# Attention's chunk loop: a chunk's loads and an inverse's loads issued one per slot instead of all in a row

## The chip, the cores and the metric

The kernel runs on one core of a Trainium2 chip. The metric is device time in microseconds (us), the median of the runs. The core has five instruction streams that matter here: TensorE (PE in the profile, with its weight loads as PEld), VectorE (DVE), ScalarE (ACT), GpSimd (POOL) and SyncE (SP), which issues most of the DMAs. Each stream works through its own instructions in order and waits on semaphores for the others.

## The reference

Two layers, each of the form x = x + mixer(LN(x)) * silu(ffn(LN(x))), on x of 2 x 1024 x 512 in float32. The change lies in the mixer of the first layer, a gated delta rule with 16 heads of 128:

```python
q = silu(conv(x @ Wq)); k = silu(conv(x @ Wk)) * 128**-0.5; v = silu(conv(x @ Wv))
alpha = sigmoid(x @ Wa + ba); beta = sigmoid(x @ Wb + bb)
def step(S, qt, kt, vt, at, bt):          # per batch and head, 1024 steps in time
    err = S @ kt - vt
    S = at * S - bt * outer(err, kt)
    return S, S @ qt
o = layernorm(o) * ln_w + ln_b
out = (o * sigmoid(x @ Wg)) @ Wo
```

The first layer's ffn has ternary weights. The second layer has a linear recurrence as its mixer and an ffn with 4-bit weights.

## The kernel before

**Chunks.** The recurrence over time is cut into 8 chunks of 128 steps. The 16 heads form 8 groups of 2; a group with both batches is 4 streams, which are worked on together. A pair of a group and a chunk is a unit, and there are 64 units. `units` (L1012) sets their order: two groups alternate, chunk by chunk, so u=0, 1, 2, 3 are (group 0, chunk 0), (1, 0), (0, 1), (1, 1), and u=16 starts groups 2 and 3, u=32 groups 4 and 5, u=48 groups 6 and 7.

**What a unit needs.** Within a chunk, the step from time to time becomes the inverse of a triangular 128 x 128 matrix, of which four 32 x 32 blocks lie on the diagonal. `ahead_k`, `ahead_e` and `ahead_l` (L671 to L726) make the keys, the decays and the triangular matrices of a group some time ahead and store them in DRAM (dk, de, dl). `invert` (L728) inverts all diagonal blocks of one group at once: it loads the blocks from dl into ll with four DMAs (L732), clears m (ml), takes 31 steps of two VectorE instructions each (tl and ml), copies the result back to ll on ScalarE in four pieces, and stores it to dl with four DMAs (L759). It is a generator: each `yield` is a place where it is left and taken up later.

`within` (L765) prepares a unit, one step ahead of its use. It loads k (tile kb, L771), four blocks of G (tile ground, L775), the decays e (tile eb, one buffer, L777) and the row decays eg (L561, called from L781), seven DMAs on SP's queue one after the other. Then GpSimd makes kg and qg, TensorE makes pk and pqk, and VectorE makes kd and at from them. GpSimd also sets eg's first column, ahead of its load.

`across` (L806) is the chain of a unit: VectorE makes rt from v and the product pks of the state, TensorE turns it (pr), and four blocks follow one another: a product zw, a subtraction rr on VectorE, a product with G, a copy w4 on ScalarE. The copies go on into wt with four DMAs for each of the first three blocks (L853, one slot later); the fourth block is copied by VectorE. The product pst of kd and wt then updates the state. `finish` (L881) makes the output po of a unit, and its normalisation.

**What sets the order.** The loop at L1096 makes one step per unit. In each step, `weave` (L1014) runs through 10 slots. A slot counts `order["slot"]` up by one, takes one step of one of two chains (the unit before in even slots, this unit in odd ones), runs what is due in this slot, and then gives TensorE its share of the other work: projections such as pwk, pwq, pwv and pgate, the products of `within` and of `ahead_l`. `later(n, ...)` (L578) puts steps off: the first by n slots, each further one by one slot more; outside the loop, when `order["loop"]` is false, it runs them at once. `Ordered` (L124) keeps this order on TensorE, VectorE, ScalarE and GpSimd. The DMAs on SP are not kept in it: a scheduler places them in SP's queue.

An inverse runs over seven steps of the loop. L1113 starts one at each u that is a multiple of 8 up to 40, for the group that comes two later, and L1117 to L1119 take it up in slots 1, 8, 9 and 10 of that step and in slots 1, 3, 5, 6, 8 and 10 of the next six. These are 40 times in all. Before the change, the first of them issues the four loads and clears m, three do nothing, 31 take the steps, four copy, and the 39th stores.

Steps are of unequal length on TensorE. In steps with u mod 4 below 2, a second projection (`tail`, L1148) is the keys of a later group, up to u=37; at u=40 and 41 there is none, and from u=44 on it is a piece of the output product for as long as that lasts.

Of the kernel before, what the change touches and what calls it, by code (L numbers as in the profile page):

```python
# [22 lines left out]
P = 128  # L23
# [7 lines left out]
NS = 4  # L31
# [25 lines left out]
def cols(ap, n):  # L57

    if len(ap.shape) == 2:
        ap = ap.unsqueeze(2)  # L60
    return ap.to_broadcast([ap.shape[0], ap.shape[1], n])
# [231 lines left out]
def first_layer(ctx, tc, a, cst, minus_half, keep, xnT, od, gd, pd, then):  # L293
# [29 lines left out]
    nc = tc.nc  # L323
# [223 lines left out]
    gr, egr = (dr.tile([NCOL, P], F32, name=n, bufs=1) for n in ("gr", "egr"))  # L547
# [10 lines left out]
    def rows(src, hg, c, dst):  # L558

        col = c * H * B + hg * NS  # L560
        nc.sync.dma_start(  # L561
            dst, src[col : col + NS, :].rearrange("s t -> (s t)").unsqueeze(0).to_broadcast([P, NS * P])
            .rearrange("p (s t) -> p s t", s=NS)
        )
# [6 lines left out]
    order = {"loop": False, "slot": 0}  # L571
# [6 lines left out]
    def later(n, *steps):  # L578


        for i, step in enumerate(steps):
            if order["loop"] and n + i:
                due.setdefault(order["slot"] + n + i, []).append(step)
            else:
                step()

    def mm(out, **kw):
        PE.matmul(out, **kw)

    def turn(out, src):  # L590
        PE.transpose(out, src, ident)
# [136 lines left out]
    def invert(hg, store):  # L728

        ll = pl.tile([P, 32, 32], F32, tag="ll", name=f"ll_{hg}")  # L730
        for bl in range(4):
            nc.sync.dma_start(  # L732
                ll[32 * bl : 32 * bl + 32],
                store["l"][:, :, :, SLOT[bl], :].rearrange("c s i t -> (c s) i t"),
            )
        m = pl.tile([P, 32, 32], F32, tag="ml", name=f"ml_{hg}")
        POOL.memset(m, 0.0)
        POOL.memset(m.rearrange("p i j -> p (i j)")[:, 0 : 32 * 32 : 33], 1.0)
        for _ in range(3):
            yield  # L740
        for i in range(31):
            shape = [P, 31 - i, i + 1]
            t = pl.tile([P, 256], F32, tag="tl", name=f"tl_{hg}_{i}", bufs=2)
            tv = t[:, : (31 - i) * (i + 1)].rearrange("p (t j) -> p t j", j=i + 1)
            DVE.tensor_tensor(
                tv,
                ll[:, i, i + 1 :].unsqueeze(2).to_broadcast(shape),
                m[:, i, : i + 1].unsqueeze(1).to_broadcast(shape),
                ALU.mult,
            )  # L750
            rest = m[:, i + 1 :, : i + 1]
            DVE.tensor_tensor(rest, rest, tv, ALU.subtract)
            yield

        for i in range(0, 32, 8):
            ACT.copy(ll[:, :, i : i + 8].rearrange("p j i -> p i j"), m[:, i : i + 8])
            yield
        for bl in range(4):
            nc.sync.dma_start(  # L759
                store["l"][:, :, :, SLOT[bl], :].rearrange("c s j i -> (c s) j i"),  # L760
                ll[32 * bl : 32 * bl + 32],
            )
        yield

    def within(hg, c, store):  # L765

        u = f"{hg}_{c}"
        half = slice((c % 2) * P, (c % 2 + 1) * P)
        q = windows[hg, c // 2]["q"][:, :, half]
        k = pools["b"].tile([P, NS, P], F32, tag="kb", name=f"kb_{u}")  # L770
        nc.sync.dma_start(k, store["k"][c // 2][:, :, half])  # L771
        G = pools["g"][:, units.index((hg, c)) % 3]
        for s in range(NS):
            r = slice(32 * s, 32 * s + 32)
            nc.sync.dma_start(G[r, :, r], store["l"][c, s])  # L775
        e = pools["b"].tile([P, NS, P], F32, tag="eb", name=f"eb_{u}", bufs=1)
        nc.sync.dma_start(e, store["e"][c])  # L777

        eg = pools["b"].tile([P, NS, P + 4], F32, tag="eg", name=f"eg_{u}", bufs=3)
        POOL.memset(eg[:, :, 0:1], 1.0)  # L780
        rows(egr, hg, c, eg[:, :, 1 : P + 1])  # L781
        kg = pools["b"].tile([P, NS, P], F32, tag="kg", name=f"kg_{u}")
        qg = pools["b"].tile([P, NS, P], F32, tag="qg", name=f"qg_{u}", bufs=3)
        later(
            5,
            lambda: POOL.tensor_tensor(kg, k, eg[:, :, 0:P], ALU.mult),
            lambda: POOL.tensor_tensor(qg, q, eg[:, :, 1 : P + 1], ALU.mult),
        )
        yield 0
        pk = pools["i"].tile([P, NS, P], F32, tag="pi", name=f"pk_{u}")  # L790
        for s in range(NS):
            turn(pk[:, s, :], k[:, s, :])

        kd = pools["b"].tile([P, NS, P], F32, tag="kd", name=f"kd_{u}", bufs=3)
        later(1, lambda: DVE.tensor_tensor(kd, pk, cols(e[:, :, P - 1 : P], P), ALU.mult))
        yield 4 * TURN

        pqk = pools["a"].tile([P, NS, P], F32, tag="pa", name=f"pqk_{u}")
        for s in range(NS):
            mm(pqk[:, s, :], lhsT=k[:, s, :], rhs=q[:, s, :], start=True, stop=True)  # L800
        at = pools["b"].tile([P, NS, P], F32, tag="at", name=f"at_{u}", bufs=3)
        later(1, lambda: DVE.tensor_tensor(at, pqk, e, ALU.mult))
        parts[hg, c] = eg, qg, kg, at, kd, G
        yield 4 * NARROW
# [156 lines left out]
    for hg in range(3):  # L961
        stores[hg] = new_store(hg)
        wk = load_weights(hg, ("wk",))
        steps = invert(hg - 1, stores[hg - 1]) if hg else iter(())
        for p in range(NP):
            for step in of_e:
                step()
            some(1)
            done(ahead_k(hg, p, wk["wk"], stores[hg]))
            loads, *of_e = ahead_e(hg, p, stores[hg])  # L970
            of_e = itertools.chain(*of_e)
            for step in loads:
                step()
            some(1)
            ell()
            for _ in zip(range(0 if hg and not p else 14), steps):
                pass
            ls.append((hg, p))
# [52 lines left out]
    with tc.issue_after(last["act"].ins):  # L1031
# [3 lines left out]
        done(made(0, 0, "v"))  # L1035
        done(made(1, 0, "q"))
        done(within(0, 0, stores[0]))
        halves = sorted(pd)

# [56 lines left out]
        for u in range(len(units) + 1):  # L1096
# [15 lines left out]
            if u % 8 == 0:  # L1112
                steps = invert(slot + 2, stores[slot + 2]) if slot + 2 < HG else none  # L1113
                if slot + 3 < HG:
                    wk = load_weights(slot + 3, ("wk",))
                    stores[slot + 3] = new_store(slot + 3)
# [12 lines left out]
            if u + 1 < len(units):  # L1129
                hg, c = units[u + 1]  # L1130
                ready = within(hg, c, stores[hg])
                other(ready, 1)
# [4 lines left out]
            if turn4 in (0, 2) and ls:  # L1137
                hg, i_ = ls[turn4 // 2]
# [596 lines left out]
```

## Time and profile before

| | |
|---|---|
| median of 3 runs | 3189.33 us (3189.05 to 3189.89) |
| profiled execution | 3191.48 us, of which the span is 3188.9 us |
| window of the chunk loop, from the span's start | about 400 to 1770 us |
| TensorE busy in that window | 1355.53 of 1370 us |
| VectorE, ScalarE, GpSimd busy in it | 965.44, 682.88, 372.22 us |
| DMA share in it | 0.43, 117 GB/s |
| DMA ll<-dl | 128 KB, 32 of them, 4.2 us from issue to landing |
| DMA ground<-dl | 40 KB, 256 of them, 2.3 us |
| DMA wt<-w | 16 KB, 768 of them, 2.0 us |
| DMA kb, eb, eg | 256 KB, 64 each, 3.5, 3.0 and 3.9 us |

The profile shows one execution. Its times are counted from the start of the span, and the median of the runs is 2.15 us below the time of the profiled execution. Busy TensorE is no proof of peak speed, since the ends of matmuls are modelled. A group of instructions is named by its line and by the tiles that it writes and reads (out<-in). Nearly all computing instructions have line 132, since a helper records them, so they are told apart by their tiles. In a list in order of time, a number in brackets is the idle time of the engine ahead of an instruction, with what ended it; SPq is SP's DMA queue.

### The profile page before, as it was taken

The numbers are of one execution on the slowest core, as the hardware profiler recorded it, in microseconds if no ns is written. First come the engines' busy times: TensorE is split into PE (matmuls) and PEld (weight loads), VectorE is DVE, ScalarE is ACT, GpSimd is POOL, SyncE is SP. The second block draws the span as 40 slices with busy tenths as digits, with TensorE's granted clock in tenths as the row PEclk, the third lists the DMA queues.
The fourth block names the chain that finished last, engine by engine and source line by source line (L and its number), as shares of the span: only waits on it lengthen the run. The fifth ranks groups of instructions, "written<-read, shape, count | busy, mean of one in ns | idle before, by whom it ended". The sixth has DMA issues, their size and how long they took to land.

```text
span 3188.9 us, 38235 instructions
## 1 busy us (share of the span) xinstructions
PE 3148.8 (99%) x12454; PEld 1950.8 (61%) x12454; DVE 2147.2 (67%) x4294; ACT 1251.4 (39%) x2269; POOL 832.4 (26%) x1210
## 2 busy tenths in 40 slices
PE   8999999999999999999999999999999999999998
PEld 6576756666666666666666644555555555555554
DVE  4557678786877878675554454677777666776676
ACT  3466555555555555434333200222222222322223
POOL 2000123222322222222222210332333333333222
PEclk9999999999999999999999999999999999999999
DMA  6244344444444443443334465010001000110014
GB/s 183 64 119 113 112 125 115 115 129 126 119 111 132 135 125 109 111 128 100 87 84 142 117 194 156 30 34 27 27 27 40 27 27 27 34 33 27 27 37 132
DMA packets 499494, 287.40 MB, mean 90 GB/s; under 512 B 207328, under 2 KB 440544, under 8 KB 499296
## 3 DMA queue, kind: packets, MB, share of 16 engines
q1 hardware_dynamic: 490432, 268.97, 29.9%
q0 software_dynamic: 6560, 11.80, 1.3%
q10 hardware_dynamic: 2304, 4.20, 0.4%
q8 instruction: 99, 1.62, 0.2%
q14 instruction: 99, 0.81, 0.1%
HBM read 183.90 MB, written 88.34 MB: 85 GB/s over the span
## 4 chain that ended last, share of the span: by engine, by line
PE 76%; DVE 5%; issue 2%; ACT 1%; DMA 1%; SPq 1%; POOL 0%; DVEq 0%; ACTq 0%; POOLq 0%
PE po L132 15%; PE pua L132 7%; PE pga L132 7%; PE pgate L132 6%; PE pwq L132 5%; PE pwv L132 5%; PE pwk L132 4%; PE zw L132 4%; PE pgc L132 3%; PE puc L132 3%; PE jpo L211 3%; PE pub L132 2%; PE pgb L132 2%; PE pr L132 2%; PE pks L132 1%
## 5 line engine op out<-in xcount | busy, mean ns | idle before, releaser
L132 DVE TENSOR_TENSOR acc<-acc,po 128x512 f32<-128x512 f32 x408 | 277.9, 681 | 208.7 <-PE po L132 207.9
L132 PEld LDWEIGHTS po<-w_d,i 128*128 128x128 f32 x1024 | 194.5, 190 | 142.6 <-issue 111.2
L132 PE MATMUL po<-w_d,i 128*128 128x256 f32 (+1 forms) x1024 | 275.4, 392 | 0.0
L132 PE MATMUL pgate<-xnT,wg 128*128 128x512 f32 x512 | 245.7, 593 | 0.0
L132 PE MATMUL pwq<-xnT,wq 128*128 128x512 f32 x512 | 245.1, 593 | 0.0
L132 PE MATMUL pwv<-xnT,wv 128*128 128x512 f32 x512 | 243.0, 594 | 1.8 <-ACT gate L132 1.8
L132 PE MATMUL pua<-xq,w_u 128*128 128x512 f32 x512 | 240.6, 592 | 0.0
L132 PE MATMUL pga<-xq,w_g 128*128 128x512 f32 x512 | 240.6, 592 | 0.0
L132 PE MATMUL pwk<-xnT,wk 128*128 128x512 f32 x512 | 237.6, 596 | 1.5 <-ACT ka L132 1.5
L132 ACT COPY g<-pga 128x512 f32<-128x512 f32 x96 | 56.2, 585 | 447.2 <-PE pga L132 432.8
L132 DVE SCALAR_TENSOR_TENSOR v<-prewv,cw,v 128x512 f32<-128x512 f32 x192 | 165.9, 865 | 63.4 <-ACT v L132 53.3
L132 PEld LDWEIGHTS po<-w_d,s 128*128 128x128 f32 x720 | 136.8, 190 | 95.4 <-issue 77.0
L132 ACT COPY w<-zw 128x128 f32<-128x128 f32 x192 | 50.6, 264 | 362.0 <-PE zw L132 362.0
L132 DVE TENSOR_TENSOR rr<-rr,zw 128x128 f32<-128x128 f32 x192 | 54.6, 284 | 199.2 <-PE zw L132 195.2
L132 PE MATMUL po<-w_d,s 128*128 128x256 f32 x720 | 184.8, 379 | 0.0
L132 ACT ACT_TABLE_LOAD x133 | 170.6, 1283 | 17.9 <-PE pr L132 11.3
L132 POOL TENSOR_TENSOR rs<-rs,minus_half 128x4 f32<-128x4 f32 x64 | 64.5, 1007 | 429.9 <-DVE rs L132 403.8
L132 POOL TENSOR_TENSOR ot<-ot,gate 128x512 f32<-128x512 f32 x64 | 85.9, 1343 | 343.4 <-ACT ot L132 313.7
L132 DVE SCALAR_TENSOR_TENSOR ka<-prewk,cw,ka 128x512 f32<-128x512 f32 x192 | 150.4, 785 | 34.9 <-ACT ka L132 23.2
L132 PEld LDWEIGHTS zw<-rr,ground 128*128 128x128 f32 x512 | 97.0, 191 | 124.5 <-issue 102.4
L132 DVE SCALAR_TENSOR_TENSOR q<-prewq,cw,q 128x512 f32<-128x512 f32 x192 | 159.8, 833 | 15.0 <-POOL eg L132 6.3
L132 PEld LDWEIGHTS zw<-w,ground 128*128 128x128 f32 x768 | 111.3, 192 | 65.6 <-issue 55.2
(248 smaller groups left out, 6661.6 us busy)
## 6 DMA issues: line engine op xcount, KB each, us to landing
e<-gr SPq DMA_DIRECT2D x64, 256.0 KB, 3.9
de<-e SPq DMA_DIRECT2D x64, 256.0 KB, 3.0
dk<-ka SPq DMA_DIRECT2D x32, 512.0 KB, 2.8
kb<-dk SPq DMA_DIRECT2D x64, 256.0 KB, 3.5
eb<-de SPq DMA_DIRECT2D x64, 256.0 KB, 3.0
eg<-egr SPq DMA_DIRECT2D x64, 256.0 KB, 3.9
od<-ot SPq DMA_DIRECT2D x64, 256.0 KB, 2.1
wt<-w SPq DMA_DIRECT2D x768, 16.0 KB, 2.0
```

The source lines that it names most:

```text
L132: i = getattr(self.engine, name)(*args, **kw)
L211: matmul(po, lhsT=ot[:, h, :], rhs=self.wo[h], start=(h == h0), stop=(h == H - 1))
```

## The change

In `invert`, each of the four loads of ll is followed by a `yield` in the loop, and the three empty turns are dropped there: the loads go out in the turns 1 to 4, m is cleared in turn 5 together with the first VectorE step, and the stores go out in turn 40. In `within`, the loads of eg, of e and of the four blocks of G are handed to `later(1, ...)`: eg one slot after k, e two slots after, the blocks three to six slots after. Before the loop both run as they did, in a row, with the row of `within` in the new order.

```diff
@@ invert @@
                 ll[32 * bl : 32 * bl + 32],
                 store["l"][:, :, :, SLOT[bl], :].rearrange("c s i t -> (c s) i t"),
             )
+            if order["loop"]:
+                yield
         m = pl.tile([P, 32, 32], F32, tag="ml", name=f"ml_{hg}")
         POOL.memset(m, 0.0)
         POOL.memset(m.rearrange("p i j -> p (i j)")[:, 0 : 32 * 32 : 33], 1.0)
-        for _ in range(3):
+        for _ in range(0 if order["loop"] else 3):
             yield
@@ within @@
-        for s in range(NS):
+        e = pools["b"].tile([P, NS, P], F32, tag="eb", name=f"eb_{u}", bufs=1)
+
+        eg = pools["b"].tile([P, NS, P + 4], F32, tag="eg", name=f"eg_{u}", bufs=3)
+        POOL.memset(eg[:, :, 0:1], 1.0)
+
+        def block(s):
             r = slice(32 * s, 32 * s + 32)
             nc.sync.dma_start(G[r, :, r], store["l"][c, s])
-        e = pools["b"].tile([P, NS, P], F32, tag="eb", name=f"eb_{u}", bufs=1)
-        nc.sync.dma_start(e, store["e"][c])
-
-        eg = pools["b"].tile([P, NS, P + 4], F32, tag="eg", name=f"eg_{u}", bufs=3)
-        POOL.memset(eg[:, :, 0:1], 1.0)
-        rows(egr, hg, c, eg[:, :, 1 : P + 1])
+
+        later(
+            1,
+            lambda: rows(egr, hg, c, eg[:, :, 1 : P + 1]),
+            lambda: nc.sync.dma_start(e, store["e"][c]),
+            *(functools.partial(block, s) for s in range(NS)),
+        )
```

## The prediction

> **What bounds the kernel.** I read the page first: engines, slices, chain.
>
> ```profile
> span 3188.9 us, 38235 instructions
> ...
> PE 3148.8 (99%) x12454; PEld 1950.8 (61%) x12454; DVE 2147.2 (67%) x4294; ACT 1251.4 (39%) x2269; POOL 832.4 (26%) x1210
> ...
> PEclk9999999999999999999999999999999999999999
> ```
>
> TensorE is busy 99% of the span, at full clock. The change keeps every matmul, in the same order (the built programs agree on that), so only waits of TensorE can be won, with the slow clock behind them. The loop on which the change works runs from about 400 to 1770 us; there the table by stretches gives TensorE 1355.5 us busy of 1370. That is 14.5 us of idle time. Two stretches also run below full clock, 1331.0 to 1337.1 at 0.51 and 1239.9 to 1245.3 at 0.68, which costs 6.1 x 0.49 + 5.4 x 0.32 = 4.7 us. Ceiling of any repair in this loop: 19.2 us, 0.6%.
>
> Next, TensorE's waits in that window, longest first (line, releaser, us in total, times, longest):
>
> ```profile
> PE pst L132 <- DMA wt<-w: 3.5, 1, 3.5
> PE pst L132 <- DVE wt L132: 2.9, 3, 1.7
> PE zw L132 <- DVE rr L132: 1.8, 3, 1.3
> ```
>
> The longest is one wait of the state product pst for the copies wt<-w. The SP queue around it, in order of time (start, us, line):
>
> ```profile
> 1318.01 1.86 SPq L720 DMA_DIRECT2D dl<-lt  x4
> 1320.50 2.70 SPq L732 DMA_DIRECT2D ll<-dl  x4
> 1323.25 3.17 SPq L775 DMA_DIRECT2D ground<-dl  x4
> 1326.52 0.55 SPq L777 DMA_DIRECT2D eb<-de  x1
> 1327.11 0.43 SPq L561 DMA_DIRECT2D eg<-egr  x1
> 1327.64 4.96 SPq L853 DMA_DIRECT2D wt<-w  x8
> ```
>
> and TensorE beside it, then the clock by stretches (us, PE, PEld, DVE, ACT, POOL, clock, DMA):
>
> ```profile
> 1331.02 2.05 PE L132 MATMUL pst<-wt,kd 128*128 128x128 f32 x8 [3.50 <-DMA wt<-w]
> ```
>
> ```profile
> 1331.00:1337.00 6.00, 5.98 (x28) 6.00 (x29) 3.82 (x9) 0.27 (x1) 3.74 (x6) 0.50 0.20 63
> 1337.00:1343.00 6.00, 6.00 (x39) 4.52 (x39) 4.18 (x18) 1.97 (x4) 0.72 (x1) 1.00 0.41 89
> ```
>
> The four ll loads of the last inverse, and a chunk's loads behind them, stand ahead of wt on SP for 7.1 us. TensorE waits 3.5 us, then runs 6 us at half clock. This is chunk step u=40; its slots hold only one projection, so they are short (TensorE's po, which opens a step, comes at 1315.5 and 1336.9).
>
> A second place is at 796 us (u=16): same row, other victim.
>
> ```profile
> 788.89 1.28 POOL L132 TENSOR_TENSOR kg<-kb,eg 128x512 f32<-128x512 f32 x1 [10.33 <-DMA eg<-egr]
> ```
>
> ```profile
> 791.47 2.66 DVE L132 SCALAR_TENSOR_TENSOR ka<-prewk,cw,ka 128x512 f32<-128x512 f32 x2 [4.37 <-POOL prewk L132]
> ```
>
> ```profile
> 795.98 0.49 PE L132 MATMUL zw<-rr,ground 128*128 128x128 f32 x2 [1.35 <-DVE rr L132]
> ```
>
> SP issued eg at 784.84, last of its row. GpSimd, in order, stood at kg; the small copies behind it kept VectorE from ka, and rr came late.
>
> **The change, part by part.**
>
> *The row at u=40.* ll ahead of wt shrinks from four issues to one, ground from four to none; kb comes in between. SP is ordered by a scheduler, and the built order there is ll x1, kb, eg, eb, wt. From 1320.50: 0.61 + 0.61 + 0.43 + 0.55 and gaps, so wt starts at 1322.8 instead of 1327.64. In the trace wt landed 3.25 us after its row began (1330.89), so now at 1326.1. TensorE reaches pst at 1327.52: the 3.50 us go, with 1.4 to spare. With them goes the half clock, 6.1 x 0.49 = 3.0. Together -6.5.
>
> Here a rule of the Trainium skill speaks against the change: "DMA: Bandwidth & Descriptors", section "Issuing engines are not separate DMA queues", says that the sequencer's time to start a DMA is usually small beside the DMA itself. By it, reordering issues would be worth about nothing. The rows say otherwise here: an ll load is 0.61 us to issue and 3.9 to land, wt 0.59 and 1.8, and ten in a row hold wt back from 1320.50 to 1327.64. By the rule this kernel would stay at 3189; I go by the rows.
>
> *The row at u=16.* eg now follows ll x1 (777.32) and kb: issue near 778.9, landing 4.05 later as in the trace, at 783.0; kg starts 5.9 us earlier, VectorE's 4.37 and TensorE's 1.35 go: -1.35. The clock stayed at 1.00 there, so nothing more.
>
> *The loop's start.* kg waited for eg (issued 407.03, landed 411.45), and 10 us later TensorE waited 1.08 for ScalarE's rt behind that chain. eg now goes out about 3.2 us earlier, but kg also moves ahead of small copies in GpSimd's order. Ends 0 and -1.08; I take -0.8, as VectorE's 1.49 wait there for GpSimd is the link that shortens.
>
> *The other chunks.* The number of DMAs is unchanged, so SP's issue time is. Mostly ground moves behind wt. ground is read a whole step later, over 20 us, against 2.3 to land: 0. Without that cover it would cost its 2.3. eb feeds kd five slots later, against 3.0: 0.
>
> *The new wait.* The inverse's loads 2 to 4 now go out in the step's last slots, and its first VectorE step moves from the last slot of the step to the first of the next, behind at. VectorE runs in order; queued behind it are rt (for TensorE's pr) and the next rr. At u=40, SP: wt to 1325.3, ground x3 to 1327.2, wt to 1329.7, ll, ground, ll, ll: the last ll starts near 1331.6 and lands, with 3.9, near 1335.5. VectorE, from 1329.5: state 1.1, three taps of v 2.7, kd 0.7, rr 0.3, at 0.7, so it arrives near 1335.0 and waits 0.5; then 0.4 of inverse and 0.7 of rt: done 1336.6. TensorE wants pr at 1341.46 - 6.5 = 1335.0. That is a loss of 1.6; with the shortest landing in that stretch (3.1) it is 1.1, and I take 1.2. Ends 0 (VectorE early, ll early) and 3.4.
>
> Here the second rule: "TensorE: Matmul & The Clock Gate", Part 1, has the clock halve only after an idle window of about 3.4 us. By it 1.6 costs 1.6. But the row at 1239.9 shows a 1.68 wait followed by a clock of 0.68 for 5.4 us, and 1.35 at 796 by none. So a wait of 1.7 costs 3.4 (the upper end), 1.2 costs 1.2. With the rule the upper end would be 1.7.
>
> At the five other inverses the slots are longer: for u=8 the same count puts the last landing at 612.3 and VectorE there at 615.7: 0. If SP ran 3 us later this cover is gone. GpSimd's clearing of ml (1.17) moves to the same slot, where GpSimd then idles 5 to 9 us: 0. The setting of eg's first column, for which SP's eg waits, comes 1.17 later; wt (2.4) is ahead of eg on SP and covers it. The inverse's stores go out one slot later, 3.04 for four; wt behind them has over 10 us: 0.
>
> *Sum.* -6.5 - 1.35 - 0.8 + 1.2 = -7.45. The profiled execution took 3191.48 (span 3188.9 and 2.6 around it), so 3184.0 for such a run (span 3181.4); the median of the runs before is 3189.33, 2.15 lower, hence **3181.9 us**, -0.23%.
>
> **Rivals.** About 0.2% (6.4 us) is what a measurement of this kernel tells from no change; my gain passes that by 1 us.
>
> *The wait moves one step on.* What leaves the row stands before the next wt. At u=41 the count puts wt at 1337.2, landed 1340.5, and pst is due at 1342.2. If SP is 3.4 us later, pst waits 1.7 and the clock halves: 3.4 back, with 1.6 at pr 3185.7. For: the margin is only 1.7. Against: the count finds SP no earlier event to wait for.
>
> *Hidden anyway, or not done.* SP's order is a scheduler's, and in many steps the built positions are as before. If wt stays late, 3189. Against: the built order at both places has changed.
>
> *Slower: the inverse's first step stalls VectorE.* If the last ll lands over 2.8 us behind VectorE's arrival (TensorE had 4.5 us from pks to pr in step u=9, of which 1.7 is work), pr waits. With 4.5 us, TensorE loses 1.7 and as much by the clock, six times: 20.4 - 8.65 = +11.8, 3201. For: an ll load took up to 6.4 us. Against: the count at u=8 leaves 3.4 us.
>
> **Numbers.** Forecast 0.46; moved on 0.20; hidden 0.12; slower 0.22. Faster by over 0.2%: 0.46; within: 0.32; slower: 0.22. Range 3176 (no new wait, 3180.7, and 4.5 of the other 10.5 us that the ceiling leaves) to 3198 (slower, with five stalls). The forecast's own range is 3177 to 3183.
>
> **What shows it.** Right: no wait of pst for wt near 1327, no half clock until 1337, kg near 783 at u=16, pr waiting under 1.4 near 1335. Wrong: VectorE idle for ll at the inverses, or pst waiting for wt one step on, or other pauses over 1.5 us that halve the clock.

## The result, and the profile after

The changed kernel takes **3184.92 us**, median of 22 runs (3182.42 to 3187.53); the kernel before, in 22 runs beside it, 3189.34 (3186.73 to 3192.11). The ratio is 0.9986 with a 95% interval of 0.998 to 0.9993: 4.4 us less, 0.14%. A second series on another chip gave 3185.07 against 3188.99, ratio 0.9986 (0.9977 to 0.9995). The forecast was 3181.9: the sign is right, the gain is 0.59 of what was forecast. The time lies in the stated range (3176 to 3198) but outside the forecast's own (3177 to 3183), and the gain is within the 0.2% to which the prediction gave 0.32. The profiled execution of the changed kernel took 3185.56.

The page of the changed kernel:

```profile
span 3183.8 us, 38225 instructions
...
PE 3146.3 (99%) x12454; PEld 1948.2 (61%) x12454; DVE 2154.3 (68%) x4294; ACT 1251.3 (39%) x2269; POOL 830.7 (26%) x1210
```

TensorE's count is unchanged and its busy time 2.5 us less. Less slow clock would give about 3.0 (4.7 less in the loop, 1.7 more in the joining stage behind it; both are shown below). The waits of TensorE in the loop (400 to 1770), longest first:

```profile
PE pst L132 <- DVE wt L132: 4.7, 4, 1.7
PE zw L132 <- ACT w L132: 3.5, 7, 1.1
```

and of the kernel before, the row that the prediction does not show:

```profile
PE zw L132 <- ACT w L132: 1.6, 4, 1.0
```

The row "pst <- DMA wt<-w: 3.5" is gone. But "pst <- DVE wt" rose from 2.9 to 4.7, and "zw <- ACT w" from 1.6 to 3.5. In the table by stretches the loop has 12.2 us of idle TensorE (1365 - 1352.8), 14.5 before: 2.3 less. No stretch of the loop is below full clock; before two were, 4.7 us together (5.2 when the stretches are cut at every 5 us, as in the table further down).

The step u=40 on SP (start, us, line), then the engines:

```profile
1316.51 0.57 SPq L732 DMA_DIRECT2D ll<-dl  x1
1317.12 0.67 SPq L773 DMA_DIRECT2D kb<-dk  x1
1317.84 0.62 SPq L561 DMA_DIRECT2D eg<-egr  x1
1318.55 0.45 SPq L787 DMA_DIRECT2D eb<-de  x1
1319.05 2.45 SPq L861 DMA_DIRECT2D wt<-w  x4
1321.59 1.87 SPq L782 DMA_DIRECT2D ground<-dl  x3
```

```profile
1322.19 1.29 POOL L132 TENSOR_TENSOR kg<-kb,eg 128x512 f32<-128x512 f32 x1 [0.39 <-DMA eg<-egr]
1322.26 3.26 DVE L132 SCALAR_TENSOR_TENSOR v<-prewv,cw,v 128x512 f32<-128x512 f32 x2 [3.02 <-ACT v L132]
1323.44 1.54 POOL L132 TENSOR_TENSOR qg<-q,eg 128x512 f32<-128x512 f32 x1
...
1325.55 1.25 DVE L132 COPY wt<-zw 32x128 f32<-32x128 f32 x4
1325.89 1.46 PE L132 MATMUL pst<-wt,kd 128*128 128x128 f32 x8 [1.72 <-DVE wt L132]
```

```profile
1331.00:1337.00 6.00, 6.00 (x34) 4.12 (x33) 4.66 (x21) 1.97 (x4) 1.11 (x2) 1.00 0.52 164
```

SP's order is the forecast one: four issues ahead of wt instead of ten (ll, ground, eb and eg before). wt's DMAs no longer hold pst, and the clock, the third number from the end, stays at 1.00. What holds pst is VectorE's own part of wt, its copies of the fourth block: they are queued behind two taps of v (a tap is one multiply-add of the convolution that makes v), and these take 3.26 us. Before the change the same two took less than half of that:

```profile
1325.61 1.54 DVE L132 SCALAR_TENSOR_TENSOR v<-prewv,cw,v 128x512 f32<-128x512 f32 x2 [3.02 <-ACT v L132]
...
1330.83 1.28 POOL L132 TENSOR_TENSOR kg<-kb,eg 128x512 f32<-128x512 f32 x1 [5.69 <-DMA wt<-w]
```

There GpSimd's kg stood still until TensorE was waiting; now eg is early, and kg and qg run beside the taps. u=32 shows the same: two taps 1.54 before (1145.96), 2.80 after (1142.36), beside kg and qg from 1141.82 to 1144.6, and a new wait of zw of 1.09 at 1150. At u=36 both kernels have it (taps 2.87, pst waits 1.68 before and 1.73 after, near 1237). So the first theory was: **SP's row at u=40 was worth what the profile said, and a part was given back because the early eg lets kg and qg slow VectorE's taps.**

### The profile page after: what moved, and what is told of

Its sections match the earlier page's. It is cut to its first block, busy times and chain, and to the rows that moved or that the text cites. A ratio compares the mean times of both kernels' runs of the same rounds, so it can differ in the third digit from the quotient of the medians.

```text
span 3183.8 us, 38225 instructions
## 1 busy us (share of the span) xinstructions
PE 3146.3 (99%) x12454; PEld 1948.2 (61%) x12454; DVE 2154.3 (68%) x4294; ACT 1251.3 (39%) x2269; POOL 830.7 (26%) x1210
## 4 chain that ended last, share of the span: by engine, by line
PE 88%; DVE 5%; DMA 2%; ACT 2%; issue 2%; SPq 1%; POOL 0%; DVEq 0%; ACTq 0%; POOLq 0%
PE po L132 17%; PE pua L132 7%; PE pga L132 7%; PE pgate L132 6%; PE pwk L132 6%; PE pwq L132 5%; PE pwv L132 5%; PE zw L132 4%; PE pgc L132 3%; PE puc L132 3%; PE jpo L211 3%; PE pu L132 2%; PE pg L132 2%; PE pr L132 2%; PE pub L132 2%; PE pgb L132 2%
```

## The experiments

Every run was timed against the kernel before on its own chip: e1 to e4 on one (before 3188.33, 39 runs), e5 to e8 on one (3190.34, 52 runs), the last three on one (3188.99, 18 runs). Differences are to that median.

**e1, the inverse's half alone** (the diff's part in invert; within as before).

> The kernel before with the inverse's half of the change alone: the four ll loads go out one a slot, a chunk's row (ground, eb, eg) stays in a row. Theory (the gain is the SP row ahead of wt at u=40, and an early eg gives part of it back): three ll issues leave the row there, 1.9 us, so wt begins near 1325.7 and pst waits 1.6 instead of 3.5; eg stays late, so kg and qg don't meet VectorE's taps of v (1.54 us for two, not 3.3), and there are no new waits at u=32. Gain 1.9, up to 4.9 if the half clock goes too, and 0.5 to 1.3 at u=16: 3183 to 3187 us. Rival (the gain lies in the chunk's row alone, ll never mattered): 3189. Rival (VectorE, in order, stands at the inverse's first step for the last ll, so that this half costs): 3190 or more, with a wait of VectorE for ll near 1335.

Measured: 3189.15 us, ratio 1.0002 (0.9994 to 1.001): no gain, the time of the first rival. The rival with VectorE at ll is out, since VectorE has no wait for ll in the trace. pst's wait did shrink, and without a collision:

```profile
1326.85 1.13 PE L132 MATMUL pst<-wt,kd 128*128 128x128 f32 x8 [0.52 <-DMA wt<-w]
```

But rr (0.49) waits right behind it, and five waits of 0.33 to 0.55 for ScalarE's w and v stand elsewhere. The loop has no slow clock in this execution. The loop's idle time is 13.6, so only 0.9 is won, less than the interval can show.

**e2, the chunk's half alone** (the diff's part in within; the inverse as before).

> The kernel before with the chunk's half of the change alone: eg, eb and the four ground blocks go out one a slot, the four ll loads stay in a row. Theory: at u=40 the order on SP is ll x4, kb, eg, eb, wt, so wt begins near 1324.8 and lands near 1328.1; pst waits 0.6 and the half clock goes; eg comes two us later than in the changed kernel, so that kg starts behind the two taps of v and these take 1.54 us. Gain 2.9 + 3.0 at u=40, 1.35 at u=16, 1.2 at the loop's start, less 1 for a collision that stays at u=32: about 3182, that is as good as the whole change or better. Rival (both halves are needed and add up): 3187. Rival (any early eg costs as much as it wins): 3189.

Measured: 3185.55, ratio 0.999 (0.9981 to 0.9998), 2.8 less. About 3182 was expected, and the trace shows one miss: kg did come behind the two taps (1325.23; taps 1.54), yet pst waits.

```profile
1322.06 2.44 SPq L859 DMA_DIRECT2D wt<-w  x4
1322.56 1.54 DVE L132 SCALAR_TENSOR_TENSOR v<-prewv,cw,v 128x512 f32<-128x512 f32 x2 [3.02 <-ACT v L132]
1324.13 1.25 DVE L132 COPY wt<-zw 32x128 f32<-32x128 f32 x4
...
1326.35 1.13 PE L132 MATMUL pst<-wt,kd 128*128 128x128 f32 x8 [1.88 <-DVE wt L132]
```

The row names VectorE, but its first copy was done at 1324.44 (a quarter of 1.25 after 1324.13), 1.9 before pst began. The view of tile wt over 1321.9 to 1324.5, which holds just these four DMAs, gives their times to landing:

```profile
DMA to landing us min/median/max: 2.8/3.5/4.2
```

At 4.2 after 1322.06 one landed at 1326.26, 0.1 before pst began. So it was the DMAs that held pst here; in the trace before, the row's first landed after 3.25.

**e3, the changed kernel with kg and qg two slots later.**

```diff
         later(
-            5,
+            7,
             lambda: POOL.tensor_tensor(kg, k, eg[:, :, 0:P], ALU.mult),
             lambda: POOL.tensor_tensor(qg, q, eg[:, :, 1 : P + 1], ALU.mult),
```

> The changed kernel with GpSimd's kg and qg put two slots later (seven and eight slots behind the step's start instead of five and six), loads as in the changed kernel. Theory (what was given back is VectorE's taps slowed beside kg and qg): the two taps of v near 1322 take 1.54 us instead of 3.26, those near 1142 1.54 instead of 2.80, those near 1234 1.54 instead of 2.87; pst's waits of 1.72 and 1.73 and zw's of 1.09 go: 4.5 us less than the changed kernel, near 3180.4. Rival (the wait of pst near 1326 is a matter of wt's own copies, not of the taps): 3185, pst still waits 1.7. Rival (kg later makes GpSimd's small copies behind it late and pks waits in the next step): 3187 or more.

Measured: **3180.46**, ratio 0.9975 (0.9966 to 0.9983), 7.9 less than before. The time is as expected, the way there only in part: at u=40 only qg moved behind the taps, kg did not.

```profile
1319.85 1.27 POOL L132 TENSOR_TENSOR kg<-kb,eg 128x512 f32<-128x512 f32 x1 [0.38 <-DMA eg<-egr]
1319.93 2.53 DVE L132 SCALAR_TENSOR_TENSOR v<-prewv,cw,v 128x512 f32<-128x512 f32 x2 [3.02 <-ACT v L132]
...
1322.83 1.46 PE L132 MATMUL pst<-wt,kd 128*128 128x128 f32 x8 [1.21 <-DVE wt L132]
...
1325.80 0.49 PE L132 MATMUL zw<-rr,ground 128*128 128x128 f32 x2 [1.08 <-DVE rr L132]
```

At u=40 nothing is won: qg now meets the third tap, rr comes late, and zw waits the 1.08 that the changed kernel does not have. What e3 wins of idle time over the changed kernel lies at other steps: its waits of zw for w are 1.7 in the loop instead of 3.5, and pst's at u=36 is 1.17 instead of 1.73.

**e5, one slot later still** (8 instead of 7).

> The changed kernel with kg and qg three slots later (eight and nine instead of five and six), one slot more than in the run before, where two slots moved only qg behind the taps of v: there the taps took 2.16 to 2.53 us for two, and pst still waited 1.17 and 1.21. Theory (taps slowed beside kg and qg are what was given back): at u=40 kg too comes behind the two taps, which take 1.54; pst's wait near 1322 goes, the one near 1234 as well: 2.4 us less than 3180.5, near 3178. Rival (kg so late is missed by pks at the next step's second slot): waits of TensorE at pks, and 3181 or more.

Measured: 3182.21, ratio 0.9975 (0.9965 to 0.9985), 8.1 less: at u=40 and u=36 the taps are as expected, the time is not better than e3's.

```profile
1321.11 1.54 DVE L132 SCALAR_TENSOR_TENSOR v<-prewv,cw,v 128x512 f32<-128x512 f32 x2 [3.03 <-ACT v L132]
...
1323.02 1.45 PE L132 MATMUL pst<-wt,kd 128*128 128x128 f32 x8 [0.40 <-DVE wt L132]
```

The three runs give the collision's price at three places, as the length of the two taps and the wait of TensorE behind them:

| | u=40: taps, pst waits | u=36: taps, pst waits | u=32: taps, zw waits |
|---|---|---|---|
| changed kernel, kg and qg beside | 3.26, 1.72 | 2.87, 1.73 | 2.80, 1.09 |
| e3, kg beside | 2.53, 1.21 | 2.32, 1.17 | 2.16, 0.45 |
| e5, neither beside | 1.54, 0.40 | 1.54, 0.40 | 1.54, none |

At u=36 the taps shorten by 0.55 and then by 0.78 and the wait by 0.56 and 0.77, at u=32 by 0.64 and the wait by 0.64, one for one; at u=40 the wait shortens by 0.7 to 0.8 of what the taps do. That the taps are what holds these waits is shown. In e5 another wait takes their place, of pr for VectorE's rt (us in the loop, times, longest):

```profile
PE pr L132 <- DVE rt L132: 4.0, 7, 1.1
```

At the longest of them, 1247.94, two taps of ka (3.01 us) ran beside kg and ot, and an instruction of the inverse (1.13 instead of 0.34) beside qg, ahead of rt in VectorE's order. So the collision has moved on in the step; the other six were not traced.

**e6, the later products alone**, in the kernel before (5 to 7 as in e3, the loads in a row).

> The kernel before with kg and qg two slots later (seven and eight), and the loads in a row as they were. It asks whether the 7.9 us of the changed kernel with later products need the change at all. Theory: the row at u=40 still holds wt, so pst's 3.50 stays, and with it the half clock when it comes; eg still goes out last, and kg is late at u=16; only the steps where eg was early enough (near 1237 and behind 1400) win, 0.6 there and 0.3 to 0.7 at two or three more: about 2 less, 3186.5. Rival (the two edits are independent, and the later products alone bring 3.5 to 4.5): 3184.5.

Measured: 3186.26, ratio 0.9986 (0.998 to 0.9993), 4.1 less, more than the expected 2: the sum with the change's 4.4 is 8.5, and together they gave 7.9 (e3). So the rival holds: the two edits are about independent, and what e3 wins over the changed kernel is not a measure of what the change gave back. In this trace the wait of 1.35 at u=16 is gone, the one of 1.04 near 1484 is 0.40, and the one at u=36 is 0.55 shorter. At u=40 the theory was right: the row is untouched, and so is the wait.

```profile
1326.67 2.04 PE L132 MATMUL pst<-wt,kd 128*128 128x128 f32 x8 [4.31 <-DMA wt<-w]
```

```profile
1326.00:1332.00 6.00, 5.33 (x25) 5.36 (x26) 3.18 (x8) 0.27 (x1) 3.92 (x6) 0.50 0.17 56
```

The half clock comes behind it, as in the kernel before.

**e4, the change at one place**: the last inverse of the loop and the chunk (5, 4), both loaded in u=40.

```diff
+            if order["loop"] and hg == 7:
                 yield
...
+        if (hg, c) == (5, 4):
             later(1, ...)
+        else:
+            for s in range(NS):
+                block(s)
+            nc.sync.dma_start(e, store["e"][c])
+            rows(egr, hg, c, eg[:, :, 1 : P + 1])
```

> The kernel before with the change in one place alone: the last of the six inverses in the loop, and the one chunk (group 5, chunk 4) that is loaded in the same step u=40; all other inverses and chunks as before. Theory: the wait of 3.50 becomes one of 1.7 behind the slowed taps and the half clock goes: 1.8 + 3.0, less 0.2, so 3184.7, as the whole change; what the change wins elsewhere (u=16, the start, 2.5) it loses elsewhere (new waits near 1150, 701, 1061, about 2). Rival (the gain is spread over the loop, with a share of each inverse): 3188.5. Rival (the half clock is a matter of luck in one execution, absent from the median): 3187.5.

Measured: 3187.98, ratio 0.9997 (0.9989 to 1.0005). The wait is much as expected (1.43, behind taps of 2.83), and there is no half clock, but the time is that of the two rivals. The loop's idle time is 12.9, 1.6 less than before; the 0.4 us of the median are below even that. The interval reaches to 3.5 us less, just short of the 3.6 expected: that this one step carries the whole gain is not borne out.

**e7, eg ahead of eb and ground, all in a row** (nothing put off).

> The kernel before with the order of a chunk's row alone changed: eg, eb, then the four ground blocks, all in a row as before, the inverse untouched; nothing is put off to other slots. Theory: eg early ends the wait at u=16 (1.35) and shortens the one at the loop's start (0.6), but at u=40 all ten issues are still ahead of wt, so pst still waits 3 us or more near 1327, and kg and qg meet the taps of v: 1.5 to 2.5 less than before, 3186.5. Rival (the early eg is the whole of the gain): 3184. Rival (an early eg costs as much as it wins): 3188.5.

Measured: 3187.56, ratio 0.9989 (0.9983 to 0.9996), 2.8 less, a little more than expected. The waits at u=16 and at the loop's start are gone; pst at u=40 still waits 2.80 for wt, with a clock of 0.72 over the 6 us from 1328. The order alone gives as much as e2 in the median (the intervals are too wide to tell more); ground behind wt is what it lacks. One thing was expected wrongly: kg does not meet the two taps near 1324 there, they take 1.54.

**e8, eg fourth of the six loads.**

```diff
         later(
             1,
-            lambda: rows(egr, hg, c, eg[:, :, 1 : P + 1]),
             lambda: nc.sync.dma_start(e, store["e"][c]),
-            *(functools.partial(block, s) for s in range(NS)),
+            *(functools.partial(block, s) for s in range(2)),
+            lambda: rows(egr, hg, c, eg[:, :, 1 : P + 1]),
+            *(functools.partial(block, s) for s in range(2, NS)),
```

> The changed kernel with eg fourth instead of first of the loads that go out one a slot (eb, two ground blocks, eg, two ground blocks). wt is as free at u=40 as in the changed kernel, only kg starts later, bound to eg's landing. Theory: the taps of v at u=32 and u=40 take 1.54 us again, pst's 1.72 and zw's 1.09 go; against it, GpSimd in order stands at kg for eg in many steps, with the small copies behind it, which costs TensorE 1 to 3 in places like u=16: 3183 to 3186. Rival (the time follows the freeing of wt alone): 3185, with pst's wait of 1.7 unchanged.

Measured: 3187.93, ratio 0.9994 (0.9985 to 1.0002), 2.4 less; not told apart from before, and less than the 3 to 6 expected. At u=40 the taps take 1.54 and pst waits 0.21; but at the loop's start pr waits 2.57, where the changed kernel has 0.26:

```profile
424.02 0.66 PE L132 MATMUL pr<-cst,rt 128*128 128x128 f32 x4 [2.57 <-ACT rt L132]
```

Idle in the loop: 14.2. So eg first instead of fourth is worth 2.3 there alone. The kernel before issued eg as late there (407.03, here 407.17) and waited 1.08; in its order GpSimd clears prewv ahead of kg, here behind it. At u=16 no wait came back. So with pst's wait all but gone the kernel is no faster than the changed one.

**The changed kernel and e3 once more, and e9**: e2 with kg and qg two slots later.

> The changed kernel once more, beside the same with later products on one chip. If the loop's idle time (14.5 to 12.2) and the mean share of slow clock (about 1 us less) are the whole gain: 3 to 4.5 us less than before. The wait of pst near 1326 is 1.7 again, for VectorE's wt; the clock behind it, and behind the fixed wait of 2.70 near 1871, is a matter of the execution.

> The changed kernel with kg and qg two slots later, once more. Theory (two edits that add up: 4.4 for the change, 4.1 for the later products alone): 7.5 to 8.5 us less than before and 3.5 to 4 less than the changed kernel on the same chip.

> The chunk's half of the change alone, with kg and qg two slots later; the inverse's loads stay in a row. Theory: eg lands two us later at u=40 than in the changed kernel, wt is 1.5 us later than there, so pst waits under 1 for it; the chunk alone gave 2.8 and the later products 4.1, so about 6.9 less than before, not better than with the inverse's loads spread (7.9). Rival (spreading ll costs more than it wins once the products are late): 9 less than before.

Measured, in this order: 3185.07, ratio 0.9986 (0.9977 to 0.9995), 3.9 less; 3180.56, ratio 0.9969 (0.9958 to 0.9981), 8.4 less; 3180.59, ratio 0.997 (0.9959 to 0.9981), 8.4 less. The first two are as expected, but e3 is 4.5 below the changed kernel, not 3.5 to 4. e9 misses: 6.9 was expected (its rival said 9, for which e3 beside it would have had to gain less), and pst waits 1.57 and not under 1, again for wt's DMAs (their row began at 1318.72, the longest took 3.5 us, and pst began at 1322.33). e3 and e9 beat both kernels, and are equal: with late products, the spread of ll adds nothing that can be seen (e1 had shown none either).

## Why the prediction was right in sign and too large

All executions together show how far the gain can be accounted for. Idle is TensorE's idle time in the loop, "slow" the time lost there by a clock below 0.97 (summed over stretches of 5 us), both of the profiled execution; "mean clock" is over all the runs of that kernel in its series, each given to 0.001, which is 3.2 us. The sum is an estimate: the idle time less than before, and the mean clock above that of before in the same series (for the changed kernel, above all 109 runs of before), times 3187.

| kernel | pst at u=40 waits | idle | slow | mean clock (of before) | sum | less than before |
|---|---|---|---|---|---|---|
| before | 3.50, DMA | 14.5 | 5.2 | | | |
| e6 | 4.31, DMA | 12.6 | 3.5 | 0.9981 (0.9980) | 2.2 | 4.1 |
| e7 | 2.80, DMA | 11.6 | 3.4 | 0.9981 (0.9980) | 3.2 | 2.8 |
| e2 | 1.88, DMA | 11.4 | 1.7 | 0.9982 (0.9983) | 2.7 | 2.8 |
| changed | 1.72 | 12.2 | 0 | 0.9986 (0.9981) | 3.9 | 4.4 |
| changed, again | 1.76 | 11.8 | 0 | 0.9987 (0.9980) | 5.0 | 3.9 |
| e4 | 1.43 | 12.9 | 0 | 0.9988 (0.9983) | 3.0 | 0.4 |
| e1 | 0.52, DMA | 13.6 | 0 | 0.9985 (0.9983) | 1.3 | -0.8 |
| e8 | 0.21 | 14.2 | 0 | 0.9986 (0.9980) | 2.2 | 2.4 |
| e3 | 1.21 | 10.0 | 0 | 0.9988 (0.9983) | 6.1 | 7.9 |
| e3, again | 1.19 | 10.0 | 0 | 0.9988 (0.9980) | 7.2 | 8.4 |
| e5 | 0.40 | 10.7 | 0 | 0.9989 (0.9980) | 6.5 | 8.1 |
| e9 | 1.57, DMA | 8.8 | 0 | 0.9989 (0.9980) | 8.4 | 8.4 |

For the changed kernel the sum is 2.2 of idle time and 1.7 of clock. Every sum lies within the interval of its kernel, e6's at the edge, but the intervals reach about 2.5 us to each side, so this is a weak test: **how the 4.4 us divide between the places is read from the traces and not shown by the times**. That the mean clock rises because of pst's wait is argued: the kernels with a wait of 1.88 to 4.31 for wt stand at 0.9980 to 0.9983, but e1, with 0.52, is at 0.9985 beside 0.9983 on its own chip.

Point by point:

- **What bounds the kernel; SP's row ahead of wt**: right, in the order and nearly in the times. wt began at 1319.05, 7.0 us after po opened the step (1312.02); forecast 7.4 (1322.8 against 1315.37), before 12.3. The first of its DMAs took 4.0 us to land and not 3.25, which still left 1.1 before TensorE reached pst (1324.17). The rule of the Trainium skill that the prediction cites ("DMA: Bandwidth & Descriptors", "Issuing engines are not separate DMA queues"), that the time to start a DMA is usually small beside the DMA, does not decide this row: one issue is about 0.6 us here beside landings of 1.7 to 4.3, but ten in a row are 7.1, and a shorter row took away the wait for wt's DMAs.
- **"The 3.50 us go, with 1.4 to spare": the step that failed.** The working asked when wt's DMAs would land, and not what else pst needs: VectorE's quarter of wt. In the trace before, this stood behind the two taps:

```profile
1327.18 1.25 DVE L132 COPY wt<-zw 32x128 f32<-32x128 f32 x4
```

Its first copy was done at 1327.49 (1327.18 and a quarter of 1.25), 0.03 ahead of the 1327.52 at which TensorE reached pst. It had no slack, and it held only as long as kg and qg were late. The taps beside them came out 1.72 longer, and pst waits 1.72: the row is worth 1.8, not 3.5. The earlier eg is in the prediction's count of SP's issues at u=40; that its readers would then run beside the taps is not. The direct cure, VectorE's copies ahead of the two taps, was not tried.
- **"With them goes the half clock, 3.0"**: it goes, and 3.0 was right for that execution; but it is not the mean. Behind pst's wait at u=40 the half clock cost 3.0 us in e6 too, 1.4 in e7, 1.7 in e2, and nothing in the nine other executions. Over all runs the mean clocks make it about 1.7. The median before lay 2.15 below the execution from which the 3.0 was taken; the prediction subtracted both.
- **u=16, -1.35**: right. kg begins at 780.14 behind an eg issued at 776.09; no wait of TensorE near 796. **The loop's start, -0.8**: 1.08 became 0.26.
- **The other chunks at 0**: wrong. The row "zw <- ACT w" grew by 1.9. Of that 1.09 is the wait at u=32, where the taps took 1.26 longer beside kg and qg, and ScalarE's pass over v and its copy w came behind them (e3 and e5 shorten both together); the waits of 0.35 or so at 701 and 1061 were not traced to their cause.
- **The new wait at pr, +1.2**: it didn't come. pr at u=41 doesn't wait, VectorE doesn't stand for ll there. The last ll began 16.0 us after po opened the step (16.2 counted), but ll landed in 3.3 us and not 3.9, and VectorE came to its first inverse step at 20.5 and not at 19.6.
- In the trace the loop did win 2.3 + 4.7 = 7.0 us, near the forecast 7.45. That is luck. The idle time's part was to be 4.45 and was 2.3: 1.72 and 1.9 were given back uncounted, and the 1.2 counted at pr was not lost. The other 4.7 is clock, of which this pair of executions has more than the medians; 1.7 of it stands behind u=36's pause, which the forecast left alone and the change does not touch (1.68 before, 1.73 after).
- **The rivals**: "moves one step on" had the right form, a new wait of 1.7 at pst, and a time of 3185.7 close to the measured; but the wait is at the same step, for VectorE and not for SP. That the time fits is luck too. "Hidden" is out, since SP's order did change. "Slower" did not show: VectorE's only wait for ll in the loop is one of 0.3, and TensorE does not wait behind it.

## What to carry to other kernels

When a wait is taken off an operation that has several inputs, list when each of the others arrives, from the trace, and with the new timing: the next one is the price. An engine that is let go earlier (GpSimd by an early eg) starts work at a new time, and what another engine runs then can take twice as long; so ask what the freed work will start ahead of. Here the same work put two slots later gave 4 us, with the change and without it, though not at the step at which it was aimed. And a clock loss of a single execution goes into a forecast at its mean over the runs, not at its size in that trace.

## What the runs showed of the hardware

**GpSimd beside VectorE.** Two taps of 128x512 (scalar_tensor_tensor, two tensor inputs from SBUF) take 1.54 us alone, 2.13 to 2.53 beside one tensor_tensor of GpSimd of the same size, 2.80 to 3.30 beside two; GpSimd's qg takes 1.54 there instead of 1.09. Taken singly, the taps are not slowed by a factor: one that starts second waits for the first. In e5:

```profile
1323.57 1.30 POOL L132 TENSOR_TENSOR kg<-kb,eg 128x512 f32<-128x512 f32 x1
1323.96 1.46 DVE L132 SCALAR_TENSOR_TENSOR v<-prewv,cw,v 128x512 f32<-128x512 f32 x1
```

kg ends at 1324.87, the tap at 1325.42, 0.55 later. In the loop of the changed kernel 52 such taps began while one tensor_tensor of GpSimd of over 0.9 us was under way, and 48 of them ended 0.55 us after its end, whatever was left of it; of the 28 that began before one, 25 took the 0.74 to 0.77 of a tap alone, and the other three had begun less than 0.1 before it. So the price is what is left of GpSimd's instruction, less about 0.2, and it falls on whichever of the two starts second. The Trainium skill, "GPSIMD Engine Reference", section "Specifications", has the two engines share their SBUF interfaces, with contention when VectorE reads two inputs from SBUF; the rows agree on the contention, and no run here shows the interfaces.

**The clock behind a pause.** The joining stage has one pause of 2.69 to 2.70 us of TensorE, for VectorE's jg, in every kernel of this study. In eight of the thirteen profiled executions the clock fell behind it, in five it did not. The kernel before and the changed one, over 5 us:

```profile
1877.74 1.10 PE L115 MATMUL ptr<-cst,jg 128*128 128x128 f32 x8 [2.69 <-DVE jg L239]
```

```profile
1871.31 1.30 PE L115 MATMUL ptr<-cst,jg 128*128 128x128 f32 x8 [2.70 <-DVE jg L239]
```

```profile
1872.00:1877.00 5.00, 5.00 (x12) 2.38 (x11) 4.20 (x8) 0.56 (x1) 0.55 (x1) 0.66 0.72 192
```

The clock is the third number from the end, 0.66; behind the first pause it stayed at 1.00. The second lost 1.7 us there. The pause of 1.68 to 1.73 at u=36 cost clock in two of the eight executions that have it. At u=40 pauses of 1.88, 2.80, 3.50 and 4.31 cost clock, and those of 1.57, 1.72 and 1.76 did not; one of 2.57 at the loop's start (e8) cost none, and neither did any shorter one in the loop. The cost comes in blocks: the clock stands at 0.50 for 3.4 us, or for 6.8 at the 3.50 and the 4.31 (1330.15 to 1336.98 in the kernel before), so that up to 1.7 or 3.4 us are lost, whatever the pause; what falls into the pause itself costs nothing. The rule of the Trainium skill ("TensorE: Matmul & The Clock Gate", Part 1), by which an idle window of about 3.4 us is needed, sets the bar too high for these rows; that the window runs on by itself, as the same part says, would fit a cost that comes and goes, but no run here tests it. The spread of one kernel's runs goes with it: of 39 runs of the kernel before on one chip, the 17 with a mean clock of 0.999 took 3187.85 on the mean, the 18 with 0.998 took 3189.44, the 4 with 0.997 took 3191.97.
